# Graph-layer kernel on one core: row-by-row loads by the sync engine for 26 chunks in place of 18

## The chip, the cores and the metric

One core of a Trainium2 chip runs one launch. The metric is the device time in microseconds (us). The kernel before took 2321.37 us, the median of 9 runs between 2318.82 and 2328.5. One execution was profiled: 2325.59 us, of which the trace covers a span of 2323.2 us.

## The reference

There are 12500 nodes with 128 float32 features, and 200000 edges sorted by destination. All layers but the first are dense.

```python
h = jnp.maximum(_layernorm(x, axis=-1), 0.0)
msgs = h[src]                                          # one row of 512 bytes for each edge
agg = segment_sum(msgs, dst, num_segments=12500)
deg = segment_sum(ones(200000), dst, num_segments=12500)
agg = agg / jnp.maximum(deg, 1.0)[:, None]
t = relu(agg @ Wg + h @ Ws + bg)                       # 128 -> 128
t = tanh(t @ W1 + b1)                                  # 128 -> 512
t = tanh(t @ W2 + b2)                                  # 512 -> 512
out = x + (t @ W3 + b3)                                # 512 -> 128
```

## The kernel before, in words

**Setup.** The normalized rows `h` are computed in pieces and written to a table `htab` in device memory. This takes about the first 110 us.

**Chunks.** The sorted edges are cut into 1563 chunks of 128 edges. For a chunk c the 128 source rows must stand in one tile, one row in each partition. `add(c)` then multiplies that tile on TensorE by a one-hot matrix of the destinations (made by VectorE in `onehot`) and so adds the rows up in PSUM, in `agg` or, at the seam of two blocks, in `edge`. The chunks are taken in order.

**Three ways for a chunk to get its rows.**

- 80 chunks are *raw*: rows of `x` are gathered before `htab` exists and normalized later. They are 8 of every 40 chunks from chunk 256 to chunk 656.
- Most chunks are *gathered*: `gather` has GpSimd (POOL) issue one indirect DMA of 128 rows from `htab`. These are the 1465 instructions of line 306. The tiles come from a pool of `AHEAD` = 44 buffers, so a gather waits for the matmuls of the chunk that is 44 gathers older.
- 18 chunks are *slow*: SyncE (SP) loads their 128 rows one by one, each with a plain DMA of 512 bytes whose source address comes from a register. `row_loads` is the generator that does so: for every 32 rows one instruction loads 32 addresses into registers (`TENSOR_LOAD`, line 336), and then follow 32 pairs of a register move and a DMA (line 302). The tiles `srows` come from a pool of 4 buffers.

**Which chunks are slow, and when their loads stand in SP's order.** The list `slow` begins with chunk `SLOW0` = 160. After each slow chunk, `EACH` chunks that are gathered come before the next one (raw chunks don't count), up to chunk 1551. The loads are spread over the gathers: the counter `behind` counts the gathered chunks that have been added, and one batch of `TOGETHER` = 4 row loads is placed in SP's order whenever `behind * 128 // (EACH * TOGETHER)` steps up, from `behind > SLOW0 - 3 * EACH` on:

```python
if not raw(c) and c not in slow:
    behind += 1
    batch = behind * P // (EACH * TOGETHER)
    if behind > SLOW0 - 3 * EACH and batch > (behind - 1) * P // (EACH * TOGETHER):
        next(loading, 0)
```

**SP's queue.** SP executes strictly in the order in which the program places things on it. Between the row loads stand, for each block of 512 nodes, the load `hb` (256 KB of `htab`, for the block's own rows), the load `xb` (256 KB of `x`, for the residual) and the store `out_dram<-o` (256 KB). `own(s)` places `hb` of block s at chunk 64(s-2)+32; TensorE turns it (`own_turned`, line 296, tile `pt<-ident,hb`) 64 chunks later.

**Blocks.** A block of 512 nodes takes 64 chunks. After the last chunk of a block come its mean and the four dense layers (`part0` to `part4`), whose matmuls (`pm<-h,w`) are threaded between the chunk matmuls. TensorE's instructions are kept in program order. At the end (`QUICK` = chunk 1312 on) the layers of the last blocks are placed by a planned clock instead of by a fixed rhythm.

Of the kernel before, what the change touches and what calls it, by code (L numbers as in the profile page):

```python
# [39 lines left out]
STEP = 40  # L40
AHEAD = 44
SLOW0 = 160
EACH = 72
TOGETHER = 4
LOADS = 32
LATE = 12
# [13 lines left out]
def windowed(ctx, tc, x, src, dst, Wg, Ws, bg, W1, b1, W2, b2, W3, b3, out, flag):  # L60
# [25 lines left out]
    for c in range(SLOW0, NCH - 12):  # L86
        if raw(c):
            continue
        if n <= 0:
            slow.append(c)  # L90
            n = EACH
        else:
# [548 lines left out]
    for c in range(NCH):  # L641
# [18 lines left out]
# [5 lines that stand above are left out]
# [409 lines left out]
```

## Time and profile before

| | |
|---|---|
| median of 9 runs | 2321.37 us |
| profiled execution, and its span | 2325.59 us, 2323.2 us |
| busy: TensorE, GpSimd, VectorE, ScalarE | 1397.7, 1463.4, 1073.2, 215.9 us |
| gathers (line 306) | 1465, 946 ns each, first at 109.5 us, last at 2264.8 us |
| row loads on SP (line 302, `srows`) | 2304 of 0.5 KB, first at 116.2 us, last at 2120.2 us |
| address loads on SP (line 336) | 72, median 1848 ns |
| DMA engines' share over the main stretch | 0.19 to 0.22 |

Times in the trace are from the span's start. "SPq" is SP's own sequence of DMA issues; an instruction's duration there is the time it holds the sequencer. "issue" in a list of waits is time in which an engine waited for nothing that the profile shows, and "remote" is a wait whose releaser the profile can't name.

### The profile page before, as it was taken

To read this page: it belongs to the slowest core of one execution; us is meant where nothing else is said; L and a number is where in the kernel's file an instruction comes from. 1 tells how busy PE (TensorE), PEld (TensorE's weight loads), DVE (VectorE), ACT (ScalarE), POOL (GpSimd) and SP (SyncE) were. 2 spreads that over 40 slices of the span, in tenths; PEclk is the share of its full clock that TensorE was granted. 3 is DMA by queue.
4 is the path that set the end of the run, shared out by engine and by line. 5 is a ranking of instruction groups with operands and counts; after the bars stand their busy time and mean duration, and the time that the engine had idled before them with its cause. 6 is when DMAs were issued, how large, how long until landed. Compare 5 with 4: busy or idle time off the path is not lost.

```text
span 2323.2 us, 19780 instructions
## 1 busy us (share of the span) xinstructions
PE 1397.7 (60%) x5212; PEld 899.2 (39%) x5212; DVE 1073.2 (46%) x661; ACT 215.9 (9%) x352; POOL 1463.4 (63%) x1553
## 2 busy tenths in 40 slices
PE   0132254666777668766755767656667667476478
PEld 0022243344444445443433434433434434243347
DVE  5924393354565555443443434434534433435242
ACT  1100000000101101000000000000000001011012
POOL 7675666666666666666666666666666665666660
PEclk9998565777788788777777777777777768588689
DMA  6721112122222222222221222212122122122210
GB/s 169 215 53 37 50 48 56 46 54 61 53 55 56 55 56 58 56 61 51 56 55 51 59 51 56 56 50 60 51 55 61 47 58 62 46 57 54 65 50 10
DMA packets 124131, 139.34 MB, mean 60 GB/s; under 512 B 32776, under 2 KB 98454, under 8 KB 123816
## 3 DMA queue, kind: packets, MB, share of 16 engines
q0 software_dynamic: 49440, 101.35, 17.2%
q1 hardware_dynamic: 71374, 33.32, 5.2%
q10 hardware_dynamic: 3196, 3.32, 0.6%
q8 instruction: 43, 0.70, 0.1%
q14 instruction: 78, 0.64, 0.1%
HBM read 125.06 MB, written 12.82 MB: 59 GB/s over the span
## 4 chain that ended last, share of the span: by engine, by line
PE 46%; issue 26%; another core or an unknown queue 11%; POOL 8%; DVE 5%; DMA 3%; ACT 1%; SPq 0%; POOLq 0%; DVEq 0%; ACTq 0%
PE pm L293 26%; PE agg L293 13%; POOL rows L306 8%; PE edge L293 6%; DMA rows<-htab,scol 2%; PE pt L296 1%; ACT h L325 1%; DMA xt<-in_x_dram 1%; DVE oh L375 1%; DVE agg L176 0%; DVE agg L183 0%; DVE cnt L385 0%; DVE xt L177 0%; DVE h L190 0%
## 5 line engine op out<-in xcount | busy, mean ns | idle before, releaser
L306 POOL DMA_INDIRECT rows<-htab,scol x1465 | 1385.5, 946 | 776.0 <-issue 330.9
L293 PE MATMUL pm<-h,w 128*128 128x512 f32 (+4 forms) x1344 | 741.5, 644 | 227.6 <-issue 127.1
L293 PE MATMUL agg<-oh,rows 128*128 128x144 f32 (+3 forms) x2098 | 465.3, 336 | 303.0 <-issue 252.9
L293 PEld LDWEIGHTS agg<-oh,rows 128*128 128x128 f32 x2098 | 402.4, 231 | 562.9 <-issue 490.5
L375 DVE TENSOR_TENSOR oh<-shared,dloc 128x1152 f32<-128x1152 f32 (+2 forms) x186 | 242.6, 1313 | 784.9 <-remote 345.4
L385 DVE TENSOR_REDUCE cnt<-oh 128x200 bf16<-128x1600 f32 (+2 forms) x186 | 522.7, 2823 | 3.3
L293 PEld LDWEIGHTS pm<-h,w 128*128 128x128 f32 x1344 | 247.6, 222 | 298.4 <-issue 184.0
L293 PE MATMUL edge<-oh,rows 128*128 128x144 f32 (+2 forms) x832 | 185.1, 330 | 113.9 <-issue 104.4
L293 PEld LDWEIGHTS edge<-oh,rows 128*128 128x128 f32 x832 | 158.8, 225 | 228.9 <-issue 214.6
L325 ACT ACTIVATE h<-pm,b2c 128x512 f32<-128x512 f32 (+4 forms) x112 | 70.8, 632 | 751.3 <-PE pm L293 231.9
L410 DVE TENSOR_SCALAR rd<-pm 128x512 f32<-128x512 f32 (+4 forms) x28 | 17.4, 621 | 188.1 <-remote 143.8
L325 ACT ACTIVATE h<-pm,b1c 128x512 f32<-128x512 f32 (+4 forms) x112 | 69.4, 632 | 361.2 <-remote 217.2
L146 POOL DMA_INDIRECT raw<-in_x_dram,rsrc x80 | 77.0, 963 | 25.7 <-issue 24.1
L412 DVE RECIPROCAL rd<-rd 128x512 f32<-128x512 f32 (+4 forms) x28 | 81.8, 2920 | 0.0
L523 DVE TENSOR_TENSOR mT<-agg,rd 128x512 f32<-128x512 f32 (+4 forms) x28 | 17.2, 616 | 131.7 <-PE agg L293 93.3
L293 PE MATMUL pm<-cnt,ones 128*128 128x200 bf16 (+7 forms) x294 | 34.2, 243 | 50.0 <-issue 47.7
L296 PE MATMUL pt<-ident,hb 128*128 128x128 f32 x98 | 22.9, 357 | 61.9 <-DMA hb<-htab 31.0
L208 PE MATMUL pm<-ident,idx_f 98*128 98x98 f32 x32 | 6.2, 376 | 74.8 <-issue 74.5
L328 ACT COPY hT<-pt 128x512 f32<-128x512 f32 (+1 forms) x25 | 14.4, 576 | 358.7 <-PE agg L293 181.6
L293 PEld LDWEIGHTS <-ones 128*128 128x128 bf16 x294 | 25.5, 109 | 57.3 <-issue 56.1
L585 DVE TENSOR_TENSOR o<-pt,xb 128x512 f32<-128x512 f32 x23 | 15.7, 684 | 58.9 <-PE agg L293 36.1
L296 PEld LDWEIGHTS pt<-ident,hb 128*128 128x128 f32 x98 | 16.2, 186 | 68.1 <-issue 63.2
(68 smaller groups left out, 523.2 us busy)
## 6 DMA issues: line engine op xcount, KB each, us to landing
srows<-htab SPq DMA_DIRECT2D x2304, 0.5 KB
rows<-htab,scol POOLq DMA_INDIRECT x1465
hb<-htab SPq DMA_DIRECT2D x24, 256.0 KB
xb<-in_x_dram SPq DMA_DIRECT2D x23, 256.0 KB
out_dram<-o SPq DMA_DIRECT2D x23, 256.0 KB
htab<-h SPq DMA_DIRECT2D x6, 896.0 KB
xt<-in_x_dram SPq DMA_DIRECT2D x5, 896.0 KB
raw<-in_x_dram,rsrc POOLq DMA_INDIRECT x80
```

What stands on the lines that cost most here:

```text
L146: nc.gpsimd.indirect_dma_start(out=t[:, j, :], out_offset=None, in_=x, in_offset=bass.IndirectOffsetOnAxis(ap=rsrc[:, g, j : j + 1], axis=0),)
L293: tc.keep_in_program_order(nc.tensor.matmul(*a, **k))
L296: tc.keep_in_program_order(nc.tensor.transpose(*a, **k))
L306: nc.gpsimd.indirect_dma_start(out=r, out_offset=None, in_=htab, in_offset=bass.IndirectOffsetOnAxis(ap=scol[:, c : c + 1], axis=0),)
L325: tc.keep_in_program_order(nc.scalar.activation(*a, **k))
L328: tc.keep_in_program_order(nc.scalar.copy(*a))
L375: nc.vector.tensor_tensor(oh[:, :k, :w], lane[:, None, :w].to_broadcast([P, k, w]), dloc[:, g * GRP : g * GRP + k][:, :, None].to_broadcas ...
L385: nc.vector.tensor_reduce(cnt[:, :n], shifted, AX.X, ALU.add)
L410: nc.vector.tensor_scalar(rd[:, :m], dg[:, :m], 1.0, None, op0=ALU.max)
L412: nc.vector.reciprocal(rd[:, :m], rd[:, :m])
L523: nc.vector.tensor_tensor(mTs[b][:, :n], acc[b][:, :n], rds.pop(b)[:, :n], op=ALU.mult)
L585: nc.vector.tensor_tensor(o[:, :whole], po[:, :whole], xb[:, :whole], op=ALU.add)
```

## The change

One constant is changed.

```diff
 SLOW0 = 160
-EACH = 72
+EACH = 50
 TOGETHER = 4
```

With it the list `slow` holds 26 chunks in place of 18: 160, 211, 270, 329, 396, ... 1464, 1515 in place of 160, 233, 322, 411, 508, ... 1408, 1481. SP has 26 x 128 = 3328 row loads and 104 address loads (before 2304 and 72), and GpSimd 1457 gathers (before 1465). A slow chunk now follows every 50 gathers in place of every 72. A batch of 4 loads is placed every 1.56 gathers in place of every 2.25, so that in program order a slow chunk's last load stands 100 gathers ahead of its use in place of 88. ScalarE issues 8 more loads of 0.5 KB in setup (`at_i`, the indices of the slow chunks), and the tile `place` made from them has 26 rows in place of 18. The number of chunk matmuls, their shapes and the dense layers are the same.

## The prediction

> **What bounds the kernel now.** I read the page's busy times first: no engine is above 63% of the span, so the bound is a rhythm between engines and has to be looked for in the long middle stretch, 300 to 1950 us. There I asked for the gathers and for the row loads, each with the filter of that window. The first line is GpSimd's, the other two are SP's; the columns are operation, count, and shortest, median and longest duration in ns:
>
> ```profile
> L306 POOL DMA_INDIRECT rows<-htab,scol x1133: 938/944/1888, 299.2 to 1949.4; - x189
> L302 SPq DMA_DIRECT2D srows<-htab x1980: 2/217/1407, 299.9 to 1949.8; - x198
> L302 SPq MOVE srows<-htab x1979: 2/29/1406, 300.1 to 1949.8; - x198
> ```
>
> So in 1650 us there are 1133 gathers, one in 1.456 us (0.944 busy and 0.30 between two that follow at once make 1.25; the rest is stalls), and 1980 row loads, one in 0.833 us, all of SP's other work included. Next came the waits of SP's own queue in the same window, in total us, times and longest:
>
> ```profile
> SPq L302 <- DMA srows<-htab: 55.7, 113, 1.4
> SPq L302 <- DVE o L585: 6.4, 3, 5.5
> SPq L302 <- PE agg L293: 0.7, 3, 0.3
> SPq L302 <- PE edge L293: 0.4, 1, 0.4
> ```
>
> SP waits 7.5 us in 1650 for another engine, and by the timeline once 27 us more for `o` (752 to 779, which the list lacks); 55.7 us are waits for its own loads. Otherwise it issues without rest. Now the balance. A slow chunk comes every 72 gathers, which last 72 x 1.456 = 104.8 us; its 128 loads cost SP 128 x 0.833 = 106.7 us. SP just fails to keep up. The timeline shows the drift: an output store stands in SP's order soon after the VectorE instruction that fills `o`, and at 549 us it went out at once, but by 1955 us SP came to it 41 us late:
>
> ```profile
> 548.90 0.67 DVE L585 TENSOR_TENSOR o<-pt,xb 128x512 f32<-128x512 f32 x1
> 549.60 0.42 SPq L302 DMA_DIRECT2D out_dram<-o  x1
> ...
> 1913.28 0.68 DVE L585 TENSOR_TENSOR o<-pt,xb 128x512 f32<-128x512 f32 x1
> 1954.83 0.41 SPq L302 DMA_DIRECT2D out_dram<-o  x1
> ```
>
> TensorE doesn't feel it yet: a block's `hb` is issued and then turned 64 chunks (some 90 us) later, and row loads are placed 88 gathers ahead of their use.
>
> **Why a load costs 0.833 us.** Its move and its DMA have medians of 29 and 217 ns, but there are stretches in which each takes 700 ns or more. From 116 to 198 us only 30 loads go out, with a median move of 700 ns, and TensorE's instructions are spaced out likewise. The same view where TensorE stands still but GpSimd goes on, and where both stand nearly still:
>
> ```profile
> L302 SPq DMA_DIRECT2D srows<-htab x29: 3/228/704, 274.9 to 289.1; - x29
> ...
> L302 SPq DMA_DIRECT2D srows<-htab x17: 2/228/373, 332.5 to 337.8; - x17
> ...
> 274.00:291.00 17.00, 0.00 (x0) 0.00 (x0) 5.99 (x5) 0.39 (x1) 10.28 (x11) 0.50 0.17 45
> ```
>
> The first line is the window 274 to 291 (29 loads in 17 us, 0.586 us each, with no matmul and 11 gathers, as the last line shows), the second 332 to 338 (17 loads in 6 us, 0.353 each). So SP is quicker when the other two wait. The profile doesn't say why.
>
> **The change part by part.**
>
> *Removed: 8 gathers.* 8 x 1.456 = 11.7 us off GpSimd's course. Their matmuls stay.
>
> *Added: 1024 row loads and 32 address loads.* Bytes are no matter: the 16 DMA engines are at 0.19 to 0.22. What counts is SP's time: 1024 x 0.833 = 853 us more at today's pace, on an engine that has 34 us to spare in 1650.
>
> *The new balance.* 50 gathers last 72.8 us; 128 loads at today's pace last 106.7 us. SP loses 34 us a cycle until something waits.
>
> *What waits first.* SP's order decides. Ahead of the `hb` of block 4 stand 384 row loads in place of 284, ahead of that of block 5 544 in place of 396. Before, these went out at 391 and 493 us and were turned at 483 and 565 us. At 0.833 us a load they now go out at 391 + 83 = 474 us, just in time, and at 493 + 123 = 616 us, 51 us late. So from about 474 us on SP sets the pace: TensorE waits at `pt<-ident,hb` about once a block; behind it wait the matmuls of all later chunks, and since these free the tiles, GpSimd stops when all 44 are full. The row loads themselves, now 100 gathers ahead, are less urgent than `hb`. What was the cover (90 us of lead) is spent once.
>
> *SP's pace then* is the unknown term. It has to fall to 72.8 / 128 = 0.569 us a load for nothing to be lost. From above: SP does 72.8 / 0.833 = 87 loads while the 50 gathers run, and the other 41 while TensorE waits, at 0.586 us (24 us, a cycle of 97) or, once GpSimd's tiles are full too, at 0.353 us (14.5 us, a cycle of 87). But that wait isn't all lost: GpSimd gets further ahead meanwhile, and its 50 gathers back to back need only 62.4 us. From below: I counted loads and gathers in the trace in windows of 80 us from 290 to 1890 us (18, without the two around the wait of 27 us). Where there is a gather less there are 6.15 loads more: loads = 434 - 6.15 x gathers; fitted the other way round, 80 us = 1.268 x gathers + 0.108 x loads. With 128 loads to 50 gathers the two give cycles of 80 and 77 us. I take 81, just above the lines, which rest on 1440 us in which all three engines run, rather than a value near the two short stops; that is 0.633 us a load. The ends I keep are 77 (0.602) and 90 (0.703), between the two bounds from above.
>
> *Sum.* At 474 us 384 loads are out and 2944 are left: 2944 x 0.633 = 1863 us, so the last goes out near 2337 us. TensorE is then about 64 chunks behind SP's place in the program, which is chunk 1413: near chunk 1480. Before, TensorE was at chunk 1481, the last slow one, at 2195.4 us, 127.8 us ahead of the span's end. 2337 + 128 = 2465 us, 142 more than the span of 2323.2. With 77 and 90 us a cycle it is 474 + 1771 + 128 = 2373 and 474 + 2069 + 128 = 2671 us. The profiled execution is 2.4 us above its span and 4.2 above the median; 2 us either way, left out.
>
> *At nothing:* the 8 `at_i` loads on ScalarE (0.263 us each, 2.1 in all, between 33 and 69 us, while `place` is first needed at 103.6 us, behind the last piece of the table; uncovered they cost 2.1 us). The operation that makes `place` took 208 ns on 18 rows and works on the rows at once. The matmuls of slow and gathered chunks are alike (286 ns).
>
> **A rule against this.** The Trainium skill, "DMA: Bandwidth & Descriptors", section "Issuing engines are not separate DMA queues", says that issuing DMAs from several engines saves only the sequencer's time to start one, usually small beside the transfer itself. Its section on the anatomy of one DMA puts dispatch at about 50 ns, for GpSimd's path. By an estimate from that figure 1024 loads would cost SP 51 us, which it would hide, and the change would gain the 11.7 us. This trace disagrees: 0.833 us of SP's time for a load of half a kilobyte.
>
> **Rivals.**
>
> *SP speeds up as needed* (faster side). When row loads get scarce everything else may slow a little and SP reach 0.569 us, as it did for 17 us without matmuls. Then only the 8 gathers count: 2323.2 - 11.7 = 2312 us. Against: in 1650 us it never held that pace beside matmuls, and it fell behind at 0.833. It decides below 0.569 us a load. 0.05; that it ends level, 0.02.
>
> *The wait is not used* (slower still). If TensorE's waits don't let SP run faster, the pace stays 0.833: 474 + 2452 + 128 = 3054 us; with the 97 us cycle it is 474 + 2231 + 128 = 2833 us. Against: the windows at 274 and 332 us. 0.11 for all beyond 90 us a cycle.
>
> *Not what it says?* SP's order in the changed program does hold 3328 row loads and GpSimd's 1457 gathers, so no chance is kept for that.
>
> **How the numbers follow.** Forecast (SP sets the pace, 77 to 90 us a cycle): 0.82. The range is 2373 to 2671, drawn in a little to 2375 and 2660. Within 0.2% (4.6 us, about what a measurement can tell from no change): 0.02. Faster: 0.05. Slower: 0.82 + 0.11 = 0.93.
>
> **What would show it.** In the profile after: 3328 row loads over nearly the whole span, 0.60 to 0.70 us each from 500 us on; TensorE waiting for `hb<-htab`, a few to some 20 us a block, from block 4 or 5 on (before: once, 31 us, at the start); gathers at about 1.6 us; the last row load near 2337 us. It is wrong if `hb` is out well ahead of its use throughout, if the stalls are on `srows` instead, or if the last row load is out by 2150 us.

## The result, and the profile after

The changed kernel took 2627.42 us, the median of 15 runs, against 2322.88 us for the kernel before on the same chip: a ratio of 1.1295 (95% interval 1.1278 to 1.1312, taken over all runs and not from the two medians), 304 us more. The forecast was 2465 us, 142 us more than the profiled span of before. The profiled execution after has a span of 2620.1 us.

From the issue of block 4's `hb`, which still came in time, to the last row load, the source view of the two lines gives (count; shortest, median and longest ns; first and last start):

```profile
L306 POOL DMA_INDIRECT rows<-htab,scol x1155: 938/944/961, 473.4 to 2482.4; - x193
...
L302 SPq MOVE srows<-htab x2944: 1/29/1419, 475.1 to 2482.1; - x197
L302 SPq DMA_DIRECT2D srows<-htab x2944: 1/228/1420, 475.1 to 2482.1; - x197
```

2944 row loads in 2007 us are 0.682 us each, or 87.3 us for the 128 of a slow chunk; 1155 gathers in 2009 us are one in 1.74 us. The list of TensorE's waits has a new first line, and that of SP's waits shows an engine that hardly ever waits for another (total us, times, longest):

```profile
PE pt L296 <- DMA hb<-htab: 523.9, 17, 41.3
...
SPq L302 <- DMA srows<-htab: 62.7, 132, 1.5
SPq L302 <- DVE o L585: 34.9, 3, 24.2
```

Before, the first of these lines stood at 31.0 us, one wait. Now TensorE stands for 524 us at the turning of 17 blocks. That is more than the 304 us lost. Part of the difference is idle time that TensorE had before and now spends in these waits: "issue" ahead of `agg` has gone from 279.0 to 168.4 us. In the costliest groups one sees what GpSimd does in TensorE's waits: it waits for TensorE to free its tiles.

```profile
L306 POOL DMA_INDIRECT rows<-htab,scol x1457 | 1379.1, 947 | 1081.0 <-PE agg L293 470.8
```

SP's lateness, read as before from a filled `o` and its store, goes on growing, here to 162 us in place of 41:

```profile
1924.95 0.68 DVE L585 TENSOR_TENSOR o<-pt,xb 128x512 f32<-128x512 f32 x1
...
2087.86 0.41 SPq L302 DMA_DIRECT2D out_dram<-o  x1
```

The chain of waits is of no use here: followed back from the end, it reaches only to 2441 us, some 7% of the span, with a 41.7 us piece of "another core or an unknown queue" at 2463 us, so SP's share of it rounds to 0%. The list of waits and the drift between two engines' positions show the bound.

### The profile page after: what moved, and what is told of

Same layout as the page of the kernel before. It is cut to its first block, busy times and chain, and to the rows that moved or that the text cites. A ratio compares the mean times of both kernels' runs of the same rounds, so it can differ in the third digit from the quotient of the medians.

```text
span 2620.1 us, 21895 instructions
## 1 busy us (share of the span) xinstructions
PE 1330.6 (51%) x5212; PEld 870.9 (33%) x5212; DVE 1072.6 (41%) x661; ACT 216.2 (8%) x352; POOL 1456.8 (56%) x1545
## 5 line engine op out<-in xcount | busy, mean ns | idle before, releaser
L293 PE MATMUL pm<-h,w 128*128 128x512 f32 (+4 forms) x1344 | 710.1, 622 | 149.8 <-issue 92.5
L293 PE MATMUL agg<-oh,rows 128*128 128x144 f32 (+3 forms) x2090 | 432.6, 328 | 207.6 <-issue 153.2
L293 PEld LDWEIGHTS agg<-oh,rows 128*128 128x128 f32 x2090 | 387.5, 226 | 444.5 <-issue 390.6
L293 PEld LDWEIGHTS pm<-h,w 128*128 128x128 f32 x1344 | 236.7, 214 | 201.8 <-issue 135.3
L293 PE MATMUL edge<-oh,rows 128*128 128x144 f32 (+2 forms) x824 | 191.1, 331 | 132.7 <-issue 123.0
L293 PEld LDWEIGHTS <-ones 128*128 128x128 bf16 x294 | 24.5, 105 | 62.5 <-issue 61.5
```

Of the source, the lines that this page charges most:

```text
L293: tc.keep_in_program_order(nc.tensor.matmul(*a, **k))
```

## The experiments

They ran on several chips. On two the kernel before took 2308 to 2309 us, much as in the profile above; on two others 1957 us. Each ratio is to the kernel before on the same chip. "SP's pace" is taken in one window, 474 to 1400 us: 926 us divided by the row-load moves in it. A move is called stretched when it lasts over 0.4 us, where the median is 29 ns, and so is a chip on which such moves are seen. In the expectations of the first four experiments, A is that SP's issuing sets the pace, B that only the place of `hb` in SP's order does, and D that TensorE's instructions slow SP.

**Is it SP's pace, or only the place of `hb` in SP's order?** The 25 `hb` loads go to ScalarE's queue:

```diff
-        sp_dma(hb[:, :k], htab[n0 : n0 + k * P, :].rearrange("(t p) d -> p t d", p=P))
+        tc.keep_in_program_order(
+            nc.scalar.dma_start(hb[:, :k], htab[n0 : n0 + k * P, :].rearrange("(t p) d -> p t d", p=P))
+        )
```

> The changed kernel (50 gathers apart), with the 24 loads of hb issued by ScalarE and not by SP. Theory A (SP's issue time is the limit, wherever TensorE happens to meet it): the waits for hb go, but SP still has 3328 row loads at about 0.68 us, and TensorE now waits for srows or for xb; only the lead between the two is won once, 36 gathers or some 50 us: 2560 to 2600 us. Rival B (only hb's place in the queue hurts): the waits vanish and the time is that of before or less, 2310 to 2340 us.

Measured: 2708.84 us, 1.1733 (1.1656 to 1.1811), slower still, which neither expectation had. `hb` is waited for only once, at the start; the row loads are waited for instead, and so is `xb`, another load in SP's queue, through the VectorE instruction that fills `o`:

```profile
PE agg L293 <- DMA srows<-htab: 290.7, 14, 35.2
PE pt L296 <- DVE o L587: 263.4, 12, 30.0
PE edge L293 <- DMA srows<-htab: 195.0, 5, 55.0
...
DVE o L587 <- DMA xb<-in_x_dram: 161.7, 12, 44.8
...
SPq L302 <- DMA hb<-htab: 37.7, 8, 11.3
```

The loss isn't one of order: take `hb` out of SP's queue and the next thing behind SP's pace is late (0.696 us a load here). The last line is new too (0.2 us, one wait, in the changed kernel): SP now waits for loads that another queue issued, so the edit cost SP time of its own. Whether this makes the extra 4% (the changed kernel took 2608.01 us on this chip) wasn't shown.

**Does TensorE's work slow SP?** Three quarters of the second layer's products are left out, 672 of TensorE's 5212 matmul records:

```diff
-            for kk in range(HM):
-                yield mm, hop if m == 0 and kk == HM - 1 else 0
-                pe.matmul(
-                    p2[:, :n], w2[:, kk, m * P : (m + 1) * P], h1[:, kk, :n], start=(kk == 0), stop=(kk == HM - 1)
-                )
+            yield mm, hop if m == 0 else 0
+            pe.matmul(p2[:, :n], w2[:, m, m * P : (m + 1) * P], h1[:, m, :n], start=True, stop=True)
```

> The changed kernel with three of the four products of the second 512x512 layer left out: 672 of TensorE's 5212 matmul records and as many weight loads less. Theory A1 (gathers slow SP): the same within 2%, 2575 to 2660 us, SP's pace 0.66 to 0.70 us a load. Rival D (TensorE's instructions slow SP): SP gains in proportion, 0.60 us a load or less, below 2520 us.

Measured: 2670.8 us, 1.1568 (1.1531 to 1.1606), pace 0.703 us. SP doesn't recover when TensorE has less to do. The kernel is even 2.4% slower than the changed one on this chip (2608.01 us, pace 0.686), which neither expectation had and which stays unexplained. The edit takes only an eighth of the matmuls; the run without gathers, below, settles the question.

**Do SP's instructions set the time at all?** One load fetches two neighbouring rows, so SP issues 64 loads a slow chunk in place of 128, and every second row of a slow chunk isn't the right one:

```diff
-                    sp_dma(rb[p : p + 1, :], hbytes[bass.ds(v, ROWB)].rearrange("(o b) -> o b", o=1))
+                    if p % 2 == 0:
+                        sp_dma(rb[p : p + 2, :], hbytes[bass.ds(v, 2 * ROWB)].rearrange("(o b) -> o b", o=2))
```

> The changed kernel with 64 loads of two neighbouring table rows (1 KB) for a slow chunk in place of 128 loads of one row; every second row of a slow chunk is therefore not the right one. The bytes are the same, SP's issues are half. Theory A (count of issues): 64 loads to 50 gathers is less than SP managed before, SP has time to spare, no wait for hb, 2290 to 2330 us. Rival C (rows or bytes landing, not issues): stays above 2550 us.

Measured: 2294.19 us, 0.994 (0.9911 to 0.9969). The whole loss is gone, and SP rests:

```profile
SPq L302 <- DVE o L586: 446.9, 20, 71.9
```

**Do the gathers slow SP?** Every second gather is left out and its chunk takes the tile of the one before:

```diff
+    last = []
...
+        if last:
+            rows_t[c] = last.pop()
+            return
...
+        last.append(r)
```

> The changed kernel with every second gather left out, its chunk using the tile of the gather before; the rows of half the gathered chunks are therefore wrong. SP's loads and TensorE's work are the same. Theory A1 (it is the stream of gathers on GpSimd that slows SP's issues, 0.33 us a load when the gathers stop and about 1.07 us while they run): SP's pace falls to 0.53 us a load or less, no long wait for hb, 2000 to 2350 us. Rival D (TensorE's instructions slow SP): the pace stays near 0.68 us and the time above 2550 us.

Measured: 1851.02 us, 0.8018. With 25 gathers to 128 loads the pace is 0.466 us. The pace was expected to fall, though not so far; the time is below the 2000 us expected, and the expectation of no long wait for `hb` failed: with 128 loads in 59.7 us SP is still the limit.

```profile
PE pt L296 <- DMA hb<-htab: 445.4, 18, 36.4
```

Then as many gathers as that, but each twice as wide, so that all the bytes are moved (the cuts leave out that the indices are halved and that 22 buffers of double width take the place of 44):

```diff
...
+    twice = htab.rearrange("(n t) d -> n (t d)", t=2)
...
+        if last:
+            rows_t[c] = last.pop()[:, D:]
+            return
-        r = rows_in.tile([P, D], F32, name="rows")
+        r = rows_in.tile([P, 2 * D], F32, name="rows")
...
-            out=r, out_offset=None, in_=htab,
+            out=r, out_offset=None, in_=twice,
...
-        rows_t[c] = r
+        rows_t[c] = r[:, :D]
+        last.append(r)
```

> The changed kernel with every second gather left out and the other gathers twice as wide: each reads 128 pieces of 1 KB (two neighbouring table rows, at halved indices) and serves two chunks. The rows of all gathered chunks are wrong; bytes of the gathers, SP's loads and TensorE's work are the same. Theory A1 by instructions (the number of gathers slows SP): SP's pace near that of the kernel with half the gathers, 0.46 us a load, and 1830 to 1950 us. A1 by bytes (the gathers' traffic slows SP): near 0.68 us a load, above 2450 us.

> Half as many gathers, each twice as wide (the second half is another chunk's, so the rows gathered are not those wanted). On a chip with steps: if SP is slowed by each gather instruction, the pace is near that with half the gathers left out, 0.46 us a load, and the ratio 0.80 to 0.85; if by the bytes that are gathered, it stays near 0.68 us and the ratio is 1.05 or more. Without steps: 0.81, as measured there.

Measured where the kernel before took 2308.89 us: 1822.31 us, 0.7897, pace 0.467 us, the same as with half the bytes. So SP feels how many gathers there are, not what they move. Whether that is the instruction or the 128 pieces that each one reads isn't separated: both were halved together. The same kernel ran first on a quicker chip: 1585.72 us, 0.8105, pace 0.416 us. Last, no gathers after the first 44:

```diff
+    kept = []
...
+        if len(kept) >= AHEAD:
+            rows_t[c] = kept[c % AHEAD]
+            return
...
+        kept.append(r)
```

> The changed kernel with the first 44 gathers alone; later chunks take their tiles again. Theory S on a chip with steps: after the first 44 gathers (some 180 us) no move over 0.4 us, row loads at 0.33 to 0.41 us each with the loads of the addresses, SP still limits: span 1400 to 1600 us. Rival U (TensorE's and SP's own load stretches the steps): 5% or more of the moves are still over 0.4 us after 200 us.

Measured: 1649.85 us, 0.7144; the span of 1648.4 us is some 50 us over what I expected. In the window 300 to 1490 us not one move is stretched:

```profile
L302 SPq DMA_DIRECT2D srows<-htab x2874: 227/228/301, 299.8 to 1489.7; - x192
L302 SPq MOVE srows<-htab x2873: 29/29/29, 300.1 to 1489.7; - x192
```

A load costs 0.414 us (with the address loads and SP's other work), 53 us a slow chunk, on a chip on which the changed kernel pays 0.68. TensorE and VectorE are busier there than in the changed kernel (654 and 590 us of the 926 from 474 to 1400 us, against 522 and 403), so their work isn't what stretches the moves: the rest is what running gathers take from SP. Whoever has only the profile of the changed kernel can see the same inside one of TensorE's waits, which ended at 1878.2 us. Windows 1840 to 1858.5 and 1860.5 to 1878, engines first (us; then PE, PEld, DVE, ACT and POOL busy and instructions; clock, DMA share, GB/s), then SP's loads in each:

```profile
1840.00:1858.50 18.50, 0.00 (x0) 0.00 (x0) 9.42 (x5) 0.00 (x0) 11.96 (x13) 0.56 0.19 50
1860.50:1878.00 17.50, 0.00 (x0) 0.00 (x0) 0.00 (x0) 0.00 (x0) 0.00 (x0) 0.50 0.11 32
```

```profile
L302 SPq DMA_DIRECT2D srows<-htab x17: 3/19/701, 1840.1 to 1857.8; - x17
L302 SPq MOVE srows<-htab x16: 3/359/703, 1840.1 to 1857.1; - x16
...
L302 SPq MOVE srows<-htab x35: 29/29/29, 1860.5 to 1874.8; - x35
L302 SPq DMA_DIRECT2D srows<-htab x35: 227/228/263, 1860.5 to 1874.8; - x35
```

TensorE does nothing in either. With 13 gathers, 17 loads go out in 18.5 us; with none, twice as many in less. VectorE stops too in the second, but it is no rival, as the run without gathers shows.

**How does the loss go with the number of slow chunks?** `EACH` alone is changed, first on a quicker chip, with

```diff
-EACH = 50
+EACH = 60
```

which makes 22 slow chunks, and with 100 in a second kernel, which makes 13 (1664 row loads; where a later expectation says 14 slow chunks and 6 more gathers, 13 and 5 are right).

> Slow chunks 60 gathers apart (22 of them, 2816 row loads, 1461 gathers). Theory A (SP's issue time sets the pace where it doesn't keep up): the cycles of the two kernels so far, 104.8 us for 72 gathers and 87.3 us for 50, give 95 us for 60, or 0.745 us a load; the last load goes out at about 2310 us and the end is near 2440 us, 1.04 to 1.06 of before. Rival E (the straight lines of the prediction, 1.268 us a gather and 0.108 us a load): 90 us a cycle, near 2360 us, 1.01 to 1.025.

> Slow chunks 100 gathers apart (13 of them, 1664 row loads, 1470 gathers). Theory A: SP needs 107 us a cycle and has 145, so it rests, and only the 5 gathers more count: 5 x 1.456 = 7 us, 1.002 to 1.004 of before. Rival E (each load costs the others 0.108 us): 640 loads less give 69 us, 0.97 to 0.98.

Measured there, with the kernel before at 1956.65 us: 1951.75 us, 0.9978 (0.9968 to 0.9987), with 22, and 1962.35 us, 1.0029 (1.0016 to 1.0041), with 13. For 22, both expectations failed; for 13, the 5 gathers more cost what theory A said. Fewer gathers were faster, and no move of the first is longer than 29 ns:

```profile
L302 SPq MOVE srows<-htab x2816: 29/29/29, 99.2 to 1795.4; - x188
```

Its waits, SP's and TensorE's:

```profile
SPq L302 <- DVE o L585: 582.4, 23, 88.2
...
PE agg L293 <- DMA rows<-htab,scol: 294.3, 456, 6.8
```

SP rests 582 us, and TensorE waits for gathered rows. This was a surprise and asked a new question: is the loss the change's own, or that of chips whose SP is stretched beside gathers? The next runs repeated the changed kernel and its neighbours until both kinds of chip had answered.

> The changed kernel once more. Theory S (SP's issuing is stretched in steps of 0.7 us on some chips and not on others, and that decides): where the kernel before takes near 1957 us and SP's moves last 29 ns with none of 700 ns, a row load costs about 0.33 us, SP rests, hb is out well ahead, and the ratio is 0.993 to 0.998 (8 gathers less, 10 us). Where the kernel before takes near 2310 us and a sixth of the moves lasts over 0.4 us, SP sets the pace and the ratio is 1.12 to 1.14. Rival T (the 3328 loads are too many for any chip): 1.1 or more on both kinds.

> 22 slow chunks (EACH = 60). Theory S: on a chip without steps 0.997 to 0.999, as measured there. On a chip with steps SP needs some 87 us for 128 loads and the 60 gathers take about as long or longer with their stalls, so that SP limits from later on: 1.03 to 1.06, about half of the change's loss. Rival T: the same ratio on both kinds of chip.

> 14 slow chunks (EACH = 100), 4 fewer than before. Theory S: without steps 1.002 to 1.004, as measured there. With steps SP has time to spare and the gathers set the pace, 6 more of them at some 1.47 us: 1.000 to 1.006; if SP's stretch was already what held the kernel before, below 0.995.

Measured where the kernel before took 2308.89 us: the changed kernel 2603.52 us, 1.1296 (1.1264 to 1.1327); 22 slow chunks 2388.85 us, 1.034 (1.0309 to 1.0371). Where it took 2307.76 us: 13 slow chunks 2306.17 us, 0.9966 (0.9944 to 0.9988), between the two expectations and resting on four of ten runs (2291 to 2296 us, the others 2305 to 2308), and the changed kernel a third time, 2608.01 us, 1.1273 (1.1235 to 1.131):

> The changed kernel a third time. Theory S (issue stretched in 0.7-us steps beside running gathers, on some chips only): on a chip where the kernel before takes near 1957 us, 0.993 to 0.998, no move over 0.4 us, hb out well ahead of its turning. On a chip where it takes near 2310 us, 1.12 to 1.14. Rival T: 1.1 or more on both.

And at last the changed kernel where the kernel before takes 1957.0 us:

> The changed kernel once more, for a chip on which the kernel before takes near 1957 us. Theory S there: 0.993 to 0.998, no move over 0.4 us, SP at rest for several hundred us, hb out well ahead. Rival T: 1.1 or more there too. Where the kernel before takes near 2310 us both say 1.12 to 1.14 and the run tells nothing new.

Measured: 1947.39 us, 0.9954 (0.9937 to 0.9971), a gain of 9.6 us. The 8 gathers that it saves, at the 1.25 us from one to the next when they follow at once, are 10 us. Its 3328 moves, and then its waits for `hb` and SP's rest:

```profile
L302 SPq MOVE srows<-htab x3328: 29/29/29, 98.0 to 1783.6; - x196
```

```profile
PE pt L296 <- DMA hb<-htab: 31.7, 1, 31.7
...
SPq L302 <- DVE o L585: 382.8, 24, 62.1
```

The same program is 13% slower on one kind of chip and 0.5% faster on the other. That the loads are too many for any chip is rejected.

**Does a second issuing engine help?** Every second group of 32 row loads is issued by ScalarE:

```diff
+                on_act = p0 // LOADS % 2 == 1
+                queue = nc.scalar if on_act else nc.sync
...
-                    sp_dma(rb[p : p + 1, :], hbytes[bass.ds(v, ROWB)].rearrange("(o b) -> o b", o=1))
+                    tc.keep_in_program_order(
+                        queue.dma_start(rb[p : p + 1, :], hbytes[bass.ds(v, ROWB)].rearrange("(o b) -> o b", o=1))
+                    )
```

> The changed kernel (50 gathers apart) with the row loads of every second group of 32 issued by ScalarE and not by SP. Theory A: SP has 64 loads to 50 gathers and keeps up as in the kernel with pairs, no waits for hb, 0.985 to 1.0 of before. Rival F (ScalarE's issues are as slow as SP's and stand in front of its activations): TensorE waits for activations, above 1.02.

> The changed kernel with every second group of 32 row loads issued by ScalarE. Theory S: without steps 0.994 to 0.998, as measured there. With steps SP has half the loads, 64 in 72.8 us, and no longer limits: 0.985 to 1.00. If ScalarE's stretched issues delay its activations, above 1.02 on a chip with steps.

Measured: 1948.1 us, 0.9957 (0.994 to 0.9974), on the quicker chip, no more than the changed kernel gains alone (0.9954); 2361.88 us, 1.022 (1.0188 to 1.0252), on the stretched one. There SP rests (371 us for `o`), and the list puts much of ScalarE's idle time ahead of its activations down to the row loads:

```profile
ACT h L325 <- DMA srows<-htab: 500.0, 59, 34.1
...
PE pm L293 <- ACT h L325: 124.3, 31, 17.0
...
PE pm L293 <- DVE total L415: 73.6, 8, 14.2
```

Most of the 13% is back. Whether ScalarE's loads make the 2.2% that are left isn't shown: TensorE's waits for the activations `h` have grown from 99.1 us before to 124.3 only. The largest new wait of TensorE's is the last line, for the reduction of the edge counts on VectorE, which the lists of before and of the changed kernel don't have; what delays that wasn't looked into. No version that keeps all the work was faster than the kernel before on both kinds of chip: 13 slow chunks gain 0.3% on the stretched ones and lose 0.3% on the quick ones; the changed kernel loses 13% on the stretched ones and gains 0.5% on the quick ones.

## Why the prediction was right in its mechanism and wrong in its size

*The first wait* was as worked out: `hb` of block 4 forecast at 474 us, in the trace at 473; it was turned at 479. Block 5's went out at 592 us, not 616, and from there each was issued some 3 us ahead of its turning.

*What waits* was right: TensorE at `pt<-ident,hb`, once a block from block 5 on, 16 to 41 us where I had said "a few to some 20"; from 474 us on a slow chunk's last row load was issued 29 to 81 us ahead of its first matmul. The runs with `hb` on ScalarE and with two rows a load confirm that SP's issuing sets the pace. None of the three signs that would have made it wrong appeared.

*SP's pace* is the term that failed in size: "I take 81, just above the lines, which rest on 1440 us in which all three engines run, rather than a value near the two short stops". It measured 87.3 us a cycle, 0.682 us a load in place of 0.633, and the last of the 2944 loads went out at 2482 us, 145 us after the forecast 2337. The tail was 138 us (2482 to 2620) in place of 128. With both, 2465 + 145 + 10 is the span of 2620. The ends kept for the cycle, 77 and 90 us, do hold the 87.3. (TensorE runs 64 chunks ahead of SP's place in the program, not "behind" it as the sum words it; the chunk near 1480 that it takes is right.)

The forecast chose between two kinds of evidence, and chose the wrong one. A regression over 80-us windows of a kernel whose engines hinder one another gave, fitted one way, 0.108 us for a load. That is less than the 0.217 us median of its own DMA issue, on the prediction's second profile line, so on an engine without rest the fit could hardly be right, and this was visible; the other line gives 80 / 434 = 0.184 us and fails likewise. Its windows held 52 to 56 gathers each, while the changed kernel has 46 in 80 us. The stretch at 332 us gave 0.353 us, and the windows with no gathers come near it (0.414 with all of SP's other work).

The prediction also misread that stretch. It says that TensorE and GpSimd "both stand nearly still" there, but only GpSimd does: in its first 4 us TensorE is busy for 2.74 and VectorE for 3.90 (columns as in the windows above):

```profile
332.00:336.00 4.00, 2.74 (x6) 1.71 (x7) 3.90 (x4) 2.98 (x5) 0.27 (x1) 0.50 0.07 20
```

So the trace of before already showed SP quick beside a working TensorE, with GpSimd at rest. The prediction took TensorE for a partner in the loss ("SP is quicker when the other two wait"); the run without gathers and the window at 1840 us (17 loads in 18.5 us, TensorE idle) reject it. Nor did SP reach 0.569 us "for 17 us without matmuls", as a rival says: it was 0.586 there, with 11 gathers.

Taken as SP's own price, with the rest laid on the gathers, the 0.353 us would have come close: 106.7 - 128 x 0.353 = 61.5 us over 72 gathers is 0.85 us a gather, and 50 of them make a cycle of 45.2 + 42.7 = 87.9 us. That it comes so close is partly luck. The same two prices give 96.4 us for 60 gathers, where 94.5 were measured, but 66.5 for 25, where it was 59.7, and 45.2 for none, where it was 53. The prediction had 87 among its bounds too, worked out another way and for another reason.

*The rivals.* "The wait is not used" (0.833 us a load kept) didn't come. "SP speeds up as needed", 11.7 us faster, has the outcome of the quicker chips, 9.6 us, though not the reason: there SP isn't sped up by scarce loads, its moves are simply not stretched. Nothing in one chip's profile told that the stretching was not in the kernel but in where it ran.

*The rule* of the Trainium skill ("DMA: Bandwidth & Descriptors", "Issuing engines are not separate DMA queues") says that issuing from several engines saves only issue time, which is usually small beside the DMA itself. On the quicker chips this case agrees: SP issues 1913 row loads in 926 us and still rests, and giving half of the row loads to ScalarE gains nothing more (0.9957 against 0.9954). On the stretched chips it doesn't: the same edit takes 2603.52 us to 2361.88. Even unhindered, a load holds SP for 29 + 228 ns, so that 1024 of them are 263 us and not the 51 of the prediction's estimate.

## What to carry to other kernels

When an engine has no rest and its instructions have a short median and a long tail, split its time into its own price, read where the suspected partner stands still, and a surcharge per instruction of the partner; check which engines really stand still there; then vary the mix. Distrust a fit that gives an operation less than it takes unhindered. And before a kernel is tuned to the last per cent by balancing two issuing engines, run it on a second chip: the best balance here (18, 13 or 26 slow chunks) depends on which one it is, though all but the 13% are differences of half a per cent or less.

## What the hardware showed that I had not expected

SP's issue is stretched on some chips, mostly in steps of about 0.7 us, and not on others, for the same program. In the window 474 to 1400 us, counted from the trace (moves over 0.4 us; on the kind of chip named):

| kernel, kind of chip | gathers | loads | us a load | moves over 0.4 us |
|---|---|---|---|---|
| before, stretched | 637 | 1100 | 0.842 | 232 |
| changed, stretched | 561 | 1367 | 0.677 | 207 |
| 22 slow chunks, stretched | 625 | 1254 | 0.738 | 235 |
| half the gathers, stretched | 393 | 1986 | 0.466 | 84 |
| gathers twice as wide, stretched | 400 | 1983 | 0.467 | 80 |
| no gathers, stretched | 0 | 2237 | 0.414 | 0 |
| gathers twice as wide, quick | 438 | 2224 | 0.416 | 0 |
| changed, quick (SP rests) | 741 | 1913 | 0.484 | 0 |

In the changed kernel, from 474 to 2482 us, 20% of the 2292 moves that start within 2 us of a running gather last over 0.4 us, and none of the 651 others. The surcharge isn't a constant per gather: with 0.414 us as the price of a load it is 0.74 us in the first row, (926 - 1100 x 0.414) / 637, or 0.70 without the 27 us in which SP waited for `o`, and 0.64 in the second, but 0.26 with half the gathers.

Open remains what stretches the issue, and whether it belongs to the chip or to its condition at the time. One chip, met twice, was stretched both times; no chip was seen in both conditions. It isn't that such a chip is slower in all: a gather's median is 944 ns and an unhindered row load's 228 ns on both kinds. The granted TensorE clock is lower there too (0.75 in the changed kernel against 0.91), but the same chip granted 0.87 once the gathers were gone, so that the clock may be a result as well as a cause.
